# A 64-graph stack of two graph layers in a software pipeline: new orders for its first and last rows, and its last norm moved to VectorE

## The chip, the cores and the metric

The kernel runs on one core of a Trainium2 chip. The metric is the device time of one execution in microseconds. A profiled execution has its own time and a span, the time from its first to its last instruction. A core has five engines with a queue each: TensorE (PE in the profile, its weight loads PEld), VectorE (DVE), ScalarE (ACT), GpSimd (POOL) and SyncE (SP), which here issues nearly all DMA transfers. Each queue runs in the order in which it was written.

## The reference, cut to what matters

There are 64 independent graphs of 256 nodes with 256 features. Each passes through two layers, all in float32:

```python
# layer 0, per graph
h = gat(x, adj, W1, a1); h = gat(h, adj, W2, a2)        # gat: softmax of masked scores @ (h @ W)
h = layernorm(x + h, g_ln1, b_ln1)
x = layernorm(h + relu(h @ w_ff1 + b_ff1) @ w_ff2 + b_ff2, g_ln2, b_ln2)
# layer 1, per graph: 8 heads of 32, 4 relations (adj has 0 and 1 only)
attn = softmax(q @ k.T / sqrt(32))
out = sum(attn * (adj == r) @ (x @ Wv[r] + bv[r]) for r in range(4)) @ Wo + bo
x = layernorm(x + out, g1, beta1)
x = layernorm(x + gelu(x @ W1 + b1) @ W2 + b2, g2, beta2)
```

The layer norm subtracts the mean of each row, multiplies by 1/sqrt(variance + 1e-5), then by g, and adds b.

## The kernel before

The work on one graph is cut into pieces, small Python functions that issue a few instructions each. A piece has a name of stage and step. Stage G is the two attention steps of layer 0 (`G.wh` products with the joint weights `wx`, `G.e`, `G.lr`, `G.ad`, `G.ex` the scores, their maximum and exponentials, `G.gA` and `G.gB` the two weighted sums). Stage F is layer 0's norm and feed-forward (`F.ha` to `F.he` are the matmuls of the first product, seven block products in place of eight; `F.hk` copies by ACT and `F.hp` adds by VectorE collect them; `F.f0` and `F.f1` are the second product) and q and k. Stage A is the attention of layer 1: `A.sc0` and `A.sc1` the scores of four heads each, then for each head `mx`, `ex`, `rz`, `sp` (VectorE, ACT, VectorE, POOL), `dt` and `dm` (a transpose by DMA and its regrouping, issued by SP), `mg` (a copy) and `pm` (times adj); `A.v` the values, `A.o` the weighted sums. Stage T is the output product `T.wo`, the third norm, the gelu feed-forward and the last norm. Every norm has the pieces `ln` (sum and statistics, VectorE), `rs` (root, POOL), `nm` (scaling to y, VectorE), and `ra` and `rb` (times g, plus b, POOL). After the first three norms y also goes through a transpose by DMA (`dt`, `dm`) and a copy (`c`) into columns, and `s` forms block sums of them.

The order in which pieces are issued is written out by hand in `PERIOD` (lines 43 to 60): one row of pieces with a lag, `A.dt10/3` meaning that in period p the piece is issued for graph p-3. Lags go from 0 to 5, so up to six graphs are in work. The loop at line 791 runs 69 periods; in the first five and the last five it uses the same row and leaves out the graphs that don't exist yet or any more:

```python
        for period in range(B + max(lag for _, lag in order)):
            ...
            for piece, lag in order:
                if do := graphs.get(period - lag, {}).pop(piece, None):
                    do()
            after(period)
```

The setup stands outside of this. `joint_weights` makes `wx` from W1, W2 and the attention vectors (one product, and VectorE products and reductions). `column_bias` (line 168) folds a norm's bias into the bias of the next product by matmuls with one column, and `scale_rows` (line 162) multiplies a norm's weight into the rows of the next weight; `differences` (line 153) makes block differences of a weight on POOL. For the first feed-forward, q and k this is written ahead of the first piece (lines 260 to 268); for the values and the second feed-forward, with the loads of their weights, it follows the rows of periods 1 and 2 (`after`, line 307). `xT` and `x` have one buffer each, `adj` four, and PSUM's eight banks are shared in turn.

Of the kernel before, what the change touches and what calls it, by code (L numbers as in the profile page):

```python
# [25 lines left out]
F32 = mybir.dt.float32  # L26
# [4 lines left out]
AF = mybir.ActivationFunctionType  # L31
ALU = mybir.AluOpType
AX = mybir.AxisListType

P = 128
# [18 lines left out]
L.x/0 F.dmA/1 T.sC/4 F.ke0/2 F.rbB/3 T.hp1/4 F.ke1/2 A.sp02/3 A.vp2/3 T.rsD/5 F.q/2 A.pm10/3  # L54
F.qe0/2 T.nmD/5 F.sB/2 T.hb/4 G.rzA/0 A.ve/3 F.qe1/2 T.hk2/4 A.vk4/3 A.sc1/2 T.hc/4 A.dm00/3
A.mx12/2 F.cA/1 A.ex12/2 A.mx10/2 F.sA/1 A.ex10/2 A.mx11/2 A.rz12/2 A.rz10/2 A.mg00/3 A.dt02/3
T.raD/5 A.pm00/3 A.dt13/3 A.ex11/2 F.ha/1 F.hb/1 A.sp12/2 A.dm02/3 G.gA0/0 F.hk1/1 F.hk2/1 T.hk3/4
F.hp1/1 G.gA1/0 T.rbD/5 G.wd0/0 A.mx13/2 F.hc/1 G.wd1/0 G.eB/0 A.sp10/2 A.mg02/3 A.dm13/3 A.dt12/2
T.out/5 A.rz11/2 T.hp3/4
""".split()  # L60


@with_exitstack
# [24 lines left out]
def binary(ctx: ExitStack, tc: tile.TileContext, t, most, out: bass.AP):  # L88

    nc = tc.nc  # L90
# [18 lines left out]
    def mm_tile(name, shape=(P, 2, 256)):  # L109
        return psum.tile(list(shape), F32, tag="mm", name=name, bufs=8)  # L110

    def nodes(i):
        return slice(i * P, (i + 1) * P)
# [48 lines left out]
    def scale_rows(w, norm):  # L162

        for c in range(KC):
            for part in w(c):
                nc.vector.tensor_scalar_mul(part, part, norm[0][:, c : c + 1])

    def column_bias(bias, norm, block, n):

        ps = mm_tile("fold", (P, n))  # L170
        for i in range(n):
            for c in range(KC):
                nc.tensor.matmul(
                    ps[:, i : i + 1], block(c, i), norm[1][:, c : c + 1],
                    start=i == 0 and c == 0, stop=i == n - 1 and c == KC - 1,
                    skip_group_check=True,
                )
        nc.vector.tensor_tensor(bias, bias, ps, ALU.add)

    def fold_ff(f, bias, norm):  # L180

        half = FC // 2
        column_bias(
            bias, norm, lambda c, i: f[:, BLOCKS[c, i // half], i % half * P : (i % half + 1) * P], FC
        )
        scale_rows(lambda c: [f[:, BLOCKS[c, h], :] for h in range(2)], norm)

    def ff_factors(name):
        return half_factors(
# [67 lines left out]
    w1, differences = ff_factors("L0_gnn_w_ff1")  # L257
    ff0 = w1, column("L0_gnn_b_ff1"), weight("L0_gnn_w_ff2", FC)
    rows = {n: row(t[n], n) for n in ("L0_gnn_g_ln1", "L0_gnn_b_ln1", "L0_gnn_b_ff2")}
    fold_ff(w1, ff0[1], norms[0])  # L260
    differences()
    norms.append((column("L0_gnn_g_ln2"), column("L0_gnn_b_ln2")))
    wk, wq = (weight(f"L1_gnn_{n}", KC) for n in ("Wk", "Wq"))
    bk, bq = column("L1_gnn_bk"), column("L1_gnn_bq")
    for w, bias in ((wk, bk), (wq, bq)):
        column_bias(bias, norms[1], lambda c, i, w=w: w[:, c, nodes(i)], KC)
        scale_rows(lambda c, w=w: [w[:, c, :]], norms[1])
    nc.gpsimd.tensor_scalar(bq, bq, QSCALE, 1.0, ALU.mult, ALU.mult)
    rows |= {n: row(t[n], n) for n in ("L0_gnn_g_ln2", "L0_gnn_b_ln2", "L1_gnn_bo")}
    rows |= {f"bv{r}": row(t["L1_gnn_bv"][r], f"bv{r}") for r in range(2)}  # L270
    bv0 = const.tile([P, KC], F32, name="col_bv0")
# [3 lines left out]
    norms.append((column("L1_gnn_g1"), column("L1_gnn_beta1")))  # L275
    late = {}

    def fold_values():

        for c in range(KC):  # L280
            one, zero = (wv[:, BLOCKS[c, h], :] for h in (1, 0))
            nc.gpsimd.tensor_tensor(one, one, zero, ALU.subtract)
        column_bias(bv0, norms[1], lambda c, i: wv[:, BLOCKS[c, 0], nodes(i)], KC)
        ps = mm_tile("fold", (P, D))
        for c in range(KC):
            nc.tensor.matmul(
                ps, norms[1][1][:, c : c + 1].to_broadcast([P, P]), wv[:, BLOCKS[c, 1], :],
                start=c == 0, stop=c == KC - 1,
            )
        join_biases(("bv1", "bv0", ALU.subtract))  # L290
        nc.vector.tensor_tensor(rows["bv1"], rows["bv1"], ps, ALU.add)
        scale_rows(lambda c: [wv[:, BLOCKS[c, h], :] for h in range(2)], norms[1])
        value_differences()

    def join_biases(*pairs):

        for b, bias, *op in pairs:
            nc.vector.tensor_tensor(rows[b], rows[b], rows[bias], *op or [ALU.add])

    def late_weights():  # L300
        w1, late["differences"] = ff_factors("L1_gnn_W1")
        late["wo"] = weight("L1_gnn_Wo", KC)
        late["ff1"] = w1, column("L1_gnn_b1"), weight("L1_gnn_W2", FC)
        for n in ("L1_gnn_g1", "L1_gnn_beta1", "L1_gnn_b2", "L1_gnn_g2", "L1_gnn_beta2"):
            rows[n] = row(t[n], n)

    def after(period):

        if period == 1:
            fold_values()  # L310
            late_weights()
            join_biases(("L0_gnn_b_ln1", "L0_gnn_b_ff2"), ("L0_gnn_b_ln2", "L1_gnn_bo"))
        elif period == 2:
            fold_ff(*late["ff1"][:2], norms[2])
            late["differences"]()
            join_biases(("L1_gnn_beta1", "L1_gnn_b2"))

    def over_nodes(name):
        return rows[name].unsqueeze(1).to_broadcast([P, NT, D])
# [31 lines left out]
        return join  # L351


    def layernorm(do, stage, key, name, src):

        tiles = {}

        def sums():
            ps, residual = src()
            acc = tiles["acc"] = work.tile([P, NT, D], F32, tag="acc", name=f"acc_{name}", bufs=2)  # L360
            nc.vector.tensor_tensor(acc, ps, residual, ALU.add)
            stats = small.tile([P, NT, 6], F32, tag="stats", name=f"stats_{name}", bufs=2)
            mv = tiles["mv"] = small.tile([P, NT, 2], F32, tag="mv", name=f"mv_{name}")
            for i in range(NT):
                nc.vector.bn_stats(stats[:, i, :], acc[:, i, :])
                nc.vector.bn_aggr(mv[:, i, :], stats[:, i, :])
            tiles["var"] = small.tile([P, NT], F32, tag="var", name=f"var_{name}")
            nc.vector.tensor_scalar_add(tiles["var"], mv[:, :, 1], EPS)

        def root():  # L370
            tiles["rstd"] = small.tile([P, NT], F32, tag="rstd", name=f"rstd_{name}")
            nc.gpsimd.tensor_tensor(tiles["rstd"], tiles["var"], neghalf, ALU.pow)

        def norm():
            y = tiles["y"] = work.tile([P, 2, KC, NT, 64], F32, tag="y", name=f"y_{name}", bufs=3)
            for i in range(NT):
                nc.vector.tensor_scalar(
                    y[:, :, :, i, :],
                    tiles["acc"][:, i, :].rearrange("p (k c d) -> p c k d", k=KC, c=2),
                    tiles["mv"][:, i, 0:1], tiles["rstd"][:, i : i + 1], ALU.subtract, ALU.mult,  # L380
                )

        do[f"{stage}.ln{key}"], do[f"{stage}.rs{key}"], do[f"{stage}.nm{key}"] = sums, root, norm
        return tiles

    def scaled(do, stage, key, name, tiles, g, b):
# [375 lines left out]
    def graph(b, do, tiles):  # L762
        a = gat(do, b, tiles)
        to_columns(do, "F", "A", f"a{b}", a, "ACT")
        scaled(do, "F", "A", f"a{b}", a, "L0_gnn_g_ln1", "L0_gnn_b_ln1")
        combine(do, "F", "A", f"a{b}", a)
        feed_forward(do, "F", f"a{b}", a, lambda: ff0, "r", AF.Relu)
        y = layernorm(do, "F", "B", f"b{b}", lambda: (a["ff"], a["res"]))
        to_columns(do, "F", "B", f"y{b}", y, "ACT")
        scaled(do, "F", "B", f"b{b}", y, "L0_gnn_g_ln2", "L0_gnn_b_ln2")  # L770
        combine(do, "F", "B", f"y{b}", y)
        heads = attention(do, b, projections(do, b, y), tiles)
        c = layernorm(do, "T", "C", f"c{b}", lambda: (heads["wo"], y["res"]))
        to_columns(do, "T", "C", f"c{b}", c, "ACT")
        scaled(do, "T", "C", f"c{b}", c, "L1_gnn_g1", "L1_gnn_beta1")
        combine(do, "T", "C", f"c{b}", c)
        feed_forward(do, "T", f"c{b}", c, lambda: late["ff1"], "ge", AF.Gelu)
        d = layernorm(do, "T", "D", f"d{b}", lambda: (c["ff"], c["res"]))
        scaled(do, "T", "D", f"d{b}", d, "L1_gnn_g2", "L1_gnn_beta2")

        def store():
            nc.sync.dma_start(out=out[b].rearrange("(t p) d -> p t d", p=P), in_=d["res"])

        do["T.out"] = store
# [2 lines left out]
    E = mybir.EngineType  # L787
    graph(0, graphs[0], tiles[0])
    order = [(piece, int(lag)) for piece, lag in (entry.split("/") for entry in PERIOD)]
    with tc.manual_schedule(engines={E.PE, E.DVE, E.Activation, E.Pool, E.SP}):  # L790
        for period in range(B + max(lag for _, lag in order)):
            if 0 < period < B:
                graphs[period] = {}
                graph(period, graphs[period], load(graphs[period], period))
            for piece, lag in order:
                if do := graphs.get(period - lag, {}).pop(piece, None):
                    do()
            after(period)
        assert not any(graphs.values()), graphs


@with_exitstack
# [289 lines left out]
```

## Time and profile before

| | |
|---|---|
| median of 3 runs | 3156.15 us (3155.87 to 3160.32) |
| the profiled execution's own time | 3158.29 us |
| its span | 3156.4 us |
| granted TensorE clock, mean | 0.986 |
| busy share of PE, DVE, ACT, POOL | 97%, 78%, 81%, 67% |
| mean busy share of the 16 DMA engines, 400 to 2800 us | 0.73 to 0.76 |

A row of the profile names the line of the kernel, the engine, the operation and the tiles that it writes and reads (buffer numbers left out, so `hX_a` stands for that tile of every graph), then counts and durations; a bracket gives the idle time of the engine just before and what ended it. In the rows `ff_a` and `ff_c` are the second products of the two feed-forwards, `hX`, `hY`, `hZ` their first products, `fold` the matmuls of `column_bias`, `wh` the product with `wx`, `res_d` the output.

### The profile page before, as it was taken

How to read it: one execution, taken by the hardware profiler on the slowest of the kernel's cores; microseconds unless marked ns; L12 is line 12 of the kernel's file. 1: busy time of each engine (PE TensorE's matmuls, PEld its weight loads, DVE VectorE, ACT ScalarE, POOL GpSimd, SP SyncE). 2: the span in 40 equal slices, each digit the busy share in tenths (PEclk: the TensorE clock that was granted, in tenths of full speed). 3: DMA queues.
4: the chain of work that ended last, by engine and by line, in shares of the span. 5: the costliest groups of instructions: out<-in, count | busy, mean ns of one | idle time of the engine just before them, and what ended most of it. 6: DMA issues, size and time to landing. Idle time of an engine off the chain costs nothing.

```text
span 3156.4 us, 64811 instructions
## 1 busy us (share of the span) xinstructions
PE 3048.8 (97%) x21734; PEld 2613.1 (83%) x21734; DVE 2459.1 (78%) x5231; ACT 2555.5 (81%) x5822; POOL 2122.4 (67%) x2990
## 2 busy tenths in 40 slices
PE   5799999999999999999999999999999999999996
PEld 4678888888888888888888888888888888888875
DVE  3578888888888888888887888888888888888763
ACT  1478888888888888888888888888888888888874
POOL 2457667667766766766766776766776676676664
PEclk8899999999999999999999999999999999999998
DMA  4477777778678677777677777777777767777663
GB/s 133 87 140 151 142 148 147 146 142 153 145 148 151 143 143 154 144 148 147 146 143 150 148 145 146 151 141 149 151 143 147 152 141 148 151 143 145 143 128 68
DMA packets 1022849, 449.14 MB, mean 142 GB/s; under 512 B 770960, under 2 KB 1020816, under 8 KB 1022512
## 3 DMA queue, kind: packets, MB, share of 16 engines
q1 hardware_dynamic: 1021248, 442.70, 70.0%
q8 instruction: 175, 2.87, 0.4%
q0 software_dynamic: 976, 1.72, 0.4%
q14 instruction: 162, 1.33, 0.1%
q10 hardware_dynamic: 288, 0.52, 0.1%
HBM read 58.87 MB, written 16.78 MB: 24 GB/s over the span
## 4 chain that ended last, share of the span: by engine, by line
PE 85%; DMA 5%; ACT 3%; DVE 3%; POOL 2%; issue 2%; SPq 0%; ACTq 0%; POOLq 0%; DVEq 0%
PE ff_a L517 13%; PE ff_c L517 12%; PE o L721 7%; PE hX_a L495 7%; PE hX_c L495 6%; PE sc L671 4%; PE vX L645 3%; PE k L632 3%; PE wo L740 3%; PE wh L544 3%; PE q L632 3%; PE gat_b L597 3%; PE hY_c L495 3%; PE gat_a L597 3%; PE hY_a L495 3%; DMA halves_p<-pairs_p 3%
## 5 line engine op out<-in xcount | busy, mean ns | idle before, releaser
L345 ACT COPY pm<-halves_p 128x1024 uint16<-128x1024 uint16 x384 | 516.6, 1346 | 119.6 <-DMA halves_p<-pairs_p 118.6
L713 DVE TENSOR_TENSOR pm<-pm,adj 128x512 f32<-128x512 f32 x512 | 465.4, 926 | 87.4 <-POOL pm L345 63.6
L517 PE MATMUL ff_c<-w_L_gnn_W,hid_c 128*128 128x256 f32 x2048 | 466.2, 381 | 8.4 <-ACT hid_c L509 8.4
L517 PE MATMUL ff_a<-w_L_gnn_w_ff,hid_a 128*128 128x256 f32 x2048 | 455.0, 380 | 2.2 <-ACT hid_a L509 2.2
L517 PEld LDWEIGHTS ff_a<-w_L_gnn_w_ff,hid_a 128*128 128x128 f32 x2048 | 390.6, 191 | 56.4 <-ACT hid_a L509 2.9
L517 PEld LDWEIGHTS ff_c<-w_L_gnn_W,hid_c 128*128 128x128 f32 x2048 | 385.9, 191 | 61.2 <-ACT hid_c L509 10.2
L721 PE MATMUL o<-pm,v 128*32 128x256 f32 x4096 | 249.9, 383 | 1.3 <-ACT pm L345 0.9
L509 ACT ACTIVATE hid_a<-hid_a,col_L_gnn_b_ff 128x256 f32<-128x256 f32 x512 | 218.4, 512 | 12.4 <-DVE hid_a L477 12.4
L345 POOL COPY pm<-halves_p 128x1024 uint16<-128x1024 uint16 x128 | 172.1, 1345 | 81.5 <-DMA halves_p<-pairs_p 74.7
L509 ACT ACTIVATE hid_c<-hid_c,col_L_gnn_b 128x256 f32<-128x256 f32 x512 | 218.3, 496 | 4.9 <-DVE hid_c L477 2.0
L721 PEld LDWEIGHTS o<-pm,v 128*32 128x32 f32 x4096 | 120.7, 110 | 98.5 <-issue 16.7
L425 POOL TENSOR_TENSOR S_a<-cols_a 128x128 f32<-128x128 f32 x128 | 58.5, 457 | 179.2 <-ACT cols_a L345 179.2
L495 PEld LDWEIGHTS hX_a<-cols_a,f_L_gnn_w_ff 128*128 128x128 f32 x1024 | 126.0, 194 | 41.4 <-DVE s_B L573 24.3
L495 PE MATMUL hX_a<-cols_a,f_L_gnn_w_ff 128*128 128x128 f32 x1024 | 144.6, 285 | 13.3 <-ACT cols_a L345 9.2
L671 PE MATMUL sc<-kT,qT 32*128 32x256 f32 x2048 | 149.1, 403 | 1.5 <-ACT qT L642 1.5
L495 PE MATMUL hX_a<-S_a,f_L_gnn_w_ff 128*128 128x128 f32 x1024 | 138.2, 278 | 9.1 <-ACT hid_a L474 9.0
L345 ACT COPY cols_y<-halves_y_y 128x1024 uint16<-128x1024 uint16 x64 | 86.5, 1352 | 74.5 <-DMA halves_y_y<-pairs_y_y 74.4
L632 PE MATMUL k<-cols_y,w_L_gnn_Wk 128*128 128x256 f32 x512 | 127.2, 393 | 18.5 <-ACT cols_y L345 18.5
L495 PE MATMUL hX_c<-S_c,f_L_gnn_W 128*128 128x128 f32 x1024 | 141.7, 281 | 2.2 <-ACT hid_c L474 2.2
L495 PEld LDWEIGHTS hX_a<-S_a,f_L_gnn_w_ff 128*128 128x128 f32 x1024 | 130.0, 192 | 16.7 <-ACT hid_a L474 12.6
L495 PEld LDWEIGHTS hX_c<-cols_c,f_L_gnn_W 128*128 128x128 f32 x1024 | 134.2, 191 | 11.6 <-ACT cols_c L345 4.2
L495 PEld LDWEIGHTS hX_c<-S_c,f_L_gnn_W 128*128 128x128 f32 x1024 | 124.2, 191 | 23.0 <-issue 19.6
(2747 smaller groups left out, 8837.6 us busy)
## 6 DMA issues: line engine op xcount, KB each, us to landing
halves_p<-pairs_p SPq DMA_DIRECT2D x1024, 128.0 KB, 3.3
xT<-in_xT SPq DMA_DIRECT2D x64, 256.0 KB, 4.0
adj<-in_adjT SPq DMA_DIRECT2D x64, 256.0 KB, 4.0
x<-in_x SPq DMA_DIRECT2D x64, 256.0 KB, 3.3
halves_y_a<-pairs_y_a SPq DMA_DIRECT2D x128, 128.0 KB, 3.3
halves_y_y<-pairs_y_y SPq DMA_DIRECT2D x128, 128.0 KB, 3.2
halves_y_c<-pairs_y_c SPq DMA_DIRECT2D x128, 128.0 KB, 3.0
out<-res_d SPq DMA_DIRECT2D x64, 256.0 KB, 2.4
```

The lines of the kernel that those rows point to most:

```text
L345: copy(into().bitcast(U16).rearrange("p (n s) -> p s n", s=2), t["halves"].rearrange("p s k q -> p s (k q)"),)
L495: nc.tensor.matmul(ps[:, f * P : (f + 1) * P], weights()[0][:, factor, f * P : (f + 1) * P], left, start=start and f == 0, stop=f == FC // ...
L509: nc.scalar.activation(tiles["hid"][:, f, :], tiles["hid"][:, f, :], func, bias=b1[:, f : f + 1])
L517: nc.tensor.matmul(tiles["ff"][:, i, :], tiles["hid"][:, f, nodes(i)], weights()[2][:, f, :], start=(f == 0), stop=(f == FC - 1),)
L544: nc.tensor.matmul(t["whp", j], tiles["xT"][:, c, nodes(j)], wx[:, c, :], start=(c == 0), stop=(c == KC - 1),)
L597: nc.tensor.matmul(ps, t["s"][:, j, nodes(i)], t["whz"][:, j, :width], start=(j == 0), stop=(j == NT - 1),)
L632: nc.tensor.matmul(t[key + "p"][:, o, :], w[:, c, nodes(o)], tiles["cols"][:, c, :], start=(c == 0), stop=(c == KC - 1),)
L645: nc.tensor.matmul(ps, left, wv[:, factor, :], start=start, stop=True, skip_group_check=True)
L671: nc.tensor.matmul(t["sc", g, hh][:, i, :], qkv["q"][hd, g, nodes(i)], qkv["k"][hd, g, :], start=True, stop=True,)
L713: nc.vector.tensor_tensor(pm[:, 1, :], pm[:, 0, :], tiles["adj"], ALU.mult)
L721: nc.tensor.matmul(ps[hh * DH : (hh + 1) * DH, :], qkv["v"][:, j, d0 : d0 + DH], t["pm", (g, hh)][:, r, j * N : (j + 1) * N], start=(r == ...
L740: nc.tensor.matmul(t["wo"][:, i, :], t["oT"][:, c, nodes(i)], late["wo"][:, c, :], start=(c == 0), stop=(c == KC - 1),)
```

## The change

There are now three orders. `START` is an order of its own for what the first five rows held: 447 entries like `F.ha:1`, a piece and its graph. Then follow 59 periods with `PERIOD`, as before but for one piece. `END` holds what the last five rows held, 466 entries with graphs counted from the end (`F.ha:-1`). The setup is cut into pieces named `S.`, which stand among START's entries: `S.f0`, `S.f1`, `S.f2` (fold, scaling and differences of the first feed-forward), `S.l0` to `S.l2` (the same of the second), `S.q0`, `S.q1` (fold and scaling for q and k, now with one PSUM tile for both), `S.v0` to `S.v3` (values), `S.lw` (loads of the late weights), `S.lr` (loads of the late rows and of one column), `S.j1`, `S.j2` (sums of bias rows). The loads of a graph are entries too, so that their place on SP's queue is free.

The last norm has other passes: `nm` computes (acc - mean) * g on VectorE, which doesn't need the root, `rb` multiplies by the root and adds b on VectorE, and `T.raD` is gone; y is not formed there.

```diff
 PERIOD = """
...
-T.raD/5 A.pm00/3 A.dt13/3 A.ex11/2 F.ha/1 F.hb/1 A.sp12/2 A.dm02/3 G.gA0/0 F.hk1/1 F.hk2/1 T.hk3/4
...
+START = """
+G.wh0:0 S.lr:0 G.away:0 G.wh1:0 L.adj:1 G.wc0:0 S.v0:0 L.xT:1 G.wc1:0 G.eA:0 G.lrA:0 G.adA:0
+S.f0:0 G.exA:0 G.rzA:0 S.f1:0 G.gA0:0 G.gA1:0 G.wd0:0 G.wd1:0 G.eB:0 G.lrB:0 G.adB:0 G.wh1:1
+G.wh0:1 G.exB:0 G.rzB:0 S.v1:0 S.f2:0 G.gB:0 G.wc0:1 L.xT:2 G.wh1:2 G.away:1 G.wc1:1 G.lnA:0
+S.q0:0 G.rsA:0 G.eA:1 G.wh0:2 G.nmA:0 G.wc0:2 F.dtA:0 G.lrA:1 G.adA:1 G.exA:1 F.dmA:0 G.rzA:1
+G.gA1:1 L.adj:2 L.xT:3 G.gA0:1 F.cA:0 S.lw:0 G.wd0:1 F.ha:0 S.v2:0 G.wc1:2 S.j1:0 F.hk1:0 F.sA:0
...
+G.wc0:3 G.rsA:1 F.dtB:0 G.nmA:1 F.dmB:0 F.cB:0 G.gA0:2 F.dtA:1 F.dmA:1 S.q1:0 S.l0:0 G.wd0:2 F.q:0
+F.k:0 F.qe0:0 F.raA:1 F.qe1:0 F.ke0:0 F.sB:0 G.wh1:3 F.ke1:0 S.l1:0 A.sc1:0 A.mx11:0 F.cA:1 F.ha:1
...
+END = """
+A.pm02:-4 A.sp11:-3 A.dm12:-3 A.dt10:-3 F.hk3:-2 A.pm01:-4 G.lrB:-1 F.raA:-2 T.hd:-5 A.mg13:-4
...
+T.ge2:-3 A.dt01:-1 T.ge3:-3 A.dm02:-1 A.pm00:-1 A.dm01:-1 T.raC:-4 T.ha:-2 T.sC:-2 A.vp2:-1
...
+T.rsD:-2 T.nmD:-3 T.rbD:-3 T.ge0:-1 T.ge1:-1 T.he:-1 T.hk4:-1 T.ge2:-1 T.ge3:-1 T.f0:-1 T.f1:-1
+T.out:-3 T.nmD:-2 T.rbC:-1 T.rbD:-2 T.lnD:-1 T.nmD:-1 T.rsD:-1 T.rbD:-1 T.out:-2 T.out:-1
...
-    fold_ff(w1, ff0[1], norms[0])
-    differences()
...
-    for w, bias in ((wk, bk), (wq, bq)):
-        column_bias(bias, norms[1], lambda c, i, w=w: w[:, c, nodes(i)], KC)
-        scale_rows(lambda c, w=w: [w[:, c, :]], norms[1])
-    nc.gpsimd.tensor_scalar(bq, bq, QSCALE, 1.0, ALU.mult, ALU.mult)
...
+    setup = {
+        "S.f2": differences, "S.q0": queries, "S.q1": scaled_queries,
+        "S.v0": value_difference, "S.v1": values, "S.v2": scaled_values, "S.v3": value_differences,
+        "S.lw": late_weights, "S.lr": late_rows, "S.l2": lambda: late["differences"](),
...
+        def weighted():
+
+            tiles["res"] = work.tile([P, NT, D], F32, tag="res", name=f"res_{name}", bufs=3)
+            for i in range(NT):
+                nc.vector.scalar_tensor_tensor(
+                    tiles["res"][:, i, :], tiles["acc"][:, i, :], tiles["mv"][:, i, 0:1],
+                    rows[last[0]], ALU.subtract, ALU.mult,
+                )
+
+        def finished():
+            for i in range(NT):
+                nc.vector.scalar_tensor_tensor(
+                    tiles["res"][:, i, :], tiles["res"][:, i, :], tiles["rstd"][:, i : i + 1],
+                    rows[last[1]], ALU.mult, ALU.add,
+                )
...
     with tc.manual_schedule(engines={E.PE, E.DVE, E.Activation, E.Pool, E.SP}):
...
+        for entry in START:
+            piece, b = entry.split(":")
+            run(piece, int(b))
+        for period in range(lags, B):
             for piece, lag in order:
...
+                run(piece, period - lag)
+        for entry in END:
+            piece, b = entry.split(":")
+            run(piece, B + int(b))
```

## The prediction

> **What bounds the kernel now.** I read the page first (shares, the 40 slices), then the busy times by stretch, then the timeline of each end, then the groups of the middle. The page:
>
> ```profile
> span 3156.4 us, 64811 instructions
> ...
> PE 3048.8 (97%) x21734; PEld 2613.1 (83%) x21734; DVE 2459.1 (78%) x5231; ACT 2555.5 (81%) x5822; POOL 2122.4 (67%) x2990
> ...
> PE   5799999999999999999999999999999999999996
> PEclk8899999999999999999999999999999999999998
> ```
>
> TensorE is full in all slices but the first three and the last. So the middle is its work, and only the ends have room. By stretch (columns: stretch, length, busy us of PE, PEld, DVE, ACT, POOL, granted clock, DMA share, GB/s):
>
> ```profile
> 0.00:30.40 30.40, 14.09 (x56) 12.82 (x57) 9.87 (x28) 1.28 (x1) 10.74 (x22) 1.00 0.70 190
> 30.40:111.97 81.57, 47.92 (x183) 38.85 (x183) 34.87 (x76) 23.20 (x59) 23.83 (x35) 0.75 0.34 83
> 111.97:213.75 101.78, 86.12 (x566) 72.59 (x567) 69.59 (x146) 67.06 (x170) 61.60 (x89) 0.90 0.66 125
> 213.75:2979.60 2765.85, 2760.32 (x19944) 2375.02 (x19943) 2251.95 (x4781) 2355.46 (x5370) 1930.10 (x2711) 1.00 0.74 147
> 2979.60:3058.50 78.90, 74.09 (x532) 61.50 (x530) 54.06 (x117) 61.67 (x133) 53.52 (x78) 0.98 0.63 128
> 3058.50:3156.40 97.90, 66.26 (x458) 52.28 (x458) 38.81 (x87) 46.85 (x93) 42.58 (x59) 0.88 0.39 81
> ```
>
> I cut at 213.75, where period 5 begins (its first matmuls are T.hd of graph 0), and at 2979.60, 59 periods later. In the timeline the undisturbed period is 46.65 us; 59 of them are 2752.4, so the middle holds 13.5 us of small waits. The start takes 213.75 us, of which busy time times clock is about 14+36+78=128 at most; the end takes 176.8 us, with 72.6+58.3=131. Together 131 us of the ends are not matmul work at full clock: the most that any order could return, and never all of it, since the first graph has nothing to overlap with and the last has nobody behind it. The lines that set the ends:
>
> ```profile
> 23.38 0.48 DVE L166 TENSOR_SCALAR f_L_gnn_w_ff<-f_L_gnn_w_ff,col_L_gnn_g_ln 128x512 f32<-128x512 f32 x1 [3.41 <-PE fold L173]
> 29.52 0.14 DVE L249 COPY wx<-wa 128x1 f32<-128x1 f32 x1
> 30.46 3.76 PE L544 MATMUL wh<-wx,xT 128*128 128x260 f32 x8
> 95.00 1.91 PE L544 MATMUL wh<-wx,xT 128*128 128x260 f32 x8
> 111.97 1.15 PE L671 MATMUL sc<-kT,qT 32*128 32x256 f32 x16 [0.99 <-ACT qT L642]
> 158.83 1.15 PE L671 MATMUL sc<-kT,qT 32*128 32x256 f32 x16 [0.50 <-ACT qT L642]
> 204.36 1.15 PE L671 MATMUL sc<-kT,qT 32*128 32x256 f32 x16
> 3128.42 1.16 PE L495 MATMUL hX_c<-cols_c,f_L_gnn_W 128*128 128x128 f32 x8 [3.77 <-ACT cols_c L345]
> ```
>
> wx, which every graph's first product needs, is finished at 29.5 because VectorE's queue holds scalings of the first feed-forward weights, which wait for a load and for the fold. Then A.sc1 of graphs 0, 1 and 2 stand 46.9 and 45.5 us apart: nearly a full period each, at 59% and 82% of a period's work. These are chains, not loads of work.
>
> **The change, part by part.**
>
> *Setup out of the front.* After the wait for adj at 15.12, VectorE has `away` (0.35), four products and four reductions (0.60 each, start to start), `most` (0.60) and small copies (0.5): 6.3 us, so wx at 21.4 and the first wh at 21.5, 9 us earlier. The fold S.f0 (6.56 us for 30 of its matmuls in the cold timeline) now stands behind e_A of graph 0, inside the 5 us that gat_a waits for the exponentials; about 1.5 sticks out. S.v1 and the wh products of graph 1 (1.9 and 1.7 us warm, twice that cold) stand before gat_b: +3. So F.ha of graph 0, at 65.4 now, comes at about 61.
>
> *From there to A.sc1:0*, 46.6 us now. The chain alone: products to second matmul 13 (the pieces at 0.9 with copies of 0.6 and adds of 0.7 between), 6.9 for F.f0 and F.f1, 12.3 from there to the columns (12.06 at 93.4 now, 13.4 at the end), 4.9 for k, q and sc (481.0 to 485.9): 37 us at full clock. Here the clock decides. The row: eight wh matmuls take 3.76 us at 30 and 1.91 at 95, and the clock in 30 to 112 is 0.75. The Trainium skill, "TensorE: Matmul & The Clock Gate", Part 1, says the array runs at half rate until it was busy for one window of about 3.4 us, and falls back after an idle one. By that rule the fillers (44 us of warm matmul work now stand ahead of A.sc1:0) keep it warm, and the piece costs 37; with the row's 0.75 kept, fillers lengthen the chain and it costs some 44. Sum by the one 3110, by the other 3117; I take 40, nearer the row's middle: A.sc1:0 at 101, 11 earlier.
>
> *Graphs 1 and 2.* In START, F.ha:1 follows A.sc1:0 and F.ha:2 follows A.sc1:1, so the same 37 us chain plus sc (1.1) sets the distance; matmul work between is 26 and 35, which fits. I take 39.5 for each, against 46.9 and 45.5: 13.4 gained. One cause is visible: POOL's differences for the second feed-forward (L155, 1.4 and 4.2 us at 124.9 to 131) hold up the scaling of the first heads, and with S.l2 they come after graph 0's heads. The last 9.4 us stay. Start: about 24.5.
>
> *Moved queues.* S.lr puts its six loads on POOL's queue at the front (0.55 to 0.9 us each, some 5 in all, a few waits for landing as at 9.12): POOL's next needed work is S.v0 and S.f2 (1.6 and 5.1 us), wanted only at 42 and 61, so nothing; without that cover, 5 us. S.lw puts six loads (2.25 MB, some 5 us of issue and 10 at the 218 GB/s of the first slice) on SP before x of graph 1 and y_b's transposes, which come 15 us later; now they also lie in front of the second layer's first transposes. Nothing; uncovered, up to 10 on graph 0. START also reorders the loads of adj, xT and x of graphs 1 to 4 on SP; they land 4.0 and 3.3 us after issue and are wanted later: nothing, 4 if one is late. S.q1 and S.l1 (4 us of VectorE) lie in the wait for columns. bq's scaling goes from POOL to VectorE, 0.2 us.
>
> *End.* END moves T's products and second matmuls of older graphs behind the last graphs' F and A. Ahead of F.ha:-1 stand 36.3 us of matmul work (counting pieces at their steady times), then the 37 us chain: A.sc1:-1 at 73.4 after the end's start, 83.9 now (3063.5): 10.5. From there to the last o, 49.4 now with 33 of work on any engine and 10 transposes; the held-back T work fills it, the chain of heads limits it: 45, 4.5 gained. The 41 us from there to the end keep their order.
>
> *The output's norm.* The last lines of the chain:
>
> ```profile
> 3147.14 0.70 POOL L372 TENSOR_TENSOR rstd_d<-var_d,neghalf 128x2 f32<-128x2 f32 x1 [11.38 <-DVE var_d L368]
> 3148.37 1.51 POOL L392 TENSOR_TENSOR res_d<-y_d,row_L_gnn_g 128x256 f32<-128x256 f32 x2 [0.53 <-DVE y_d L377]
> 3149.95 1.26 POOL L399 TENSOR_TENSOR res_d<-res_d,row_L_gnn_beta 128x512 f32<-128x512 f32 x1
> ```
>
> Now: root, y_d, two products, one add, store at 3151.24. After: the first VectorE pass runs beside the root, the second ends at about 3148.7: 2.5 us gained at the end. End: about 17.5.
>
> *In the middle* each graph loses 3.2 us on POOL (2x957 + 1277 ns) and two scalings on VectorE (543 ns), and gains four two-input passes of 128x256. No row shows them; the nearest is the 128x512 one (groups of 412 to 2800), s_B 682 ns and s_A 953 beside POOL:
>
> ```profile
> L573 DVE SCALAR_TENSOR_TENSOR s_A<-s_A 128x512 f32<-128x512 f32 x51 | 48.6, 953 | 5.9 <-ACT s_A L568 5.9
> L573 DVE SCALAR_TENSOR_TENSOR s_B<-s_B 128x512 f32<-128x512 f32 x51 | 34.8, 682 | 0.0
> ```
>
> Half of it with its fixed part is 0.41 (as v<-v,vX, 128x256), 0.57 contended: +0.55 to +1.2 per graph. VectorE is idle 8.7 of 46.9 us. "SBUF — State Buffer" of the skill, on the shared port pair, speaks against the change: a VectorE op with two SBUF inputs and a POOL op that reads exclude each other for the whole instruction. By it each pass may stand 1.28 us behind an add, +5.7 per graph; by the row +1.2. The second pass sits before A.mx13, and hid_a's adds behind it feed F.he, which has 2.1 us of slack, and 0.7 more from an add's own wait: 2.8. By the row the pair takes 1.1, and nothing shows; I take zero. Below zero the POOL relief could remove some of the 13.5 us of waits, but those are ACT's waits for DMA, so at most 3.
>
> **Sum.** 24.5+17.5+0 = 42 off the profiled span of 3156.4. The profiled execution took 3158.3, 1.9 outside the span and 2.1 above the median of the runs; the saving goes on the median 3156.15: 3114.
>
> **Rivals.**
> - *Chains as now (A), 0.48*: 3114, own range 3099 to 3128.
> - *The ends pack better (B), 0.24*: work alone allows it. From A.sc1:0 on the start has 69.6 busy us on VectorE and 67.1 on ACT (third stretch), and by count 69 of matmuls, in 101.8; at 92% that is 76, with A.sc1:0 at 97: start 40 off, end 30 off, 3086. Against it: the 37 us chain three times in a row.
> - *Cold clock and in-order waits (C), 0.18*: setup folds hold gat_b and q in the cold array, spacing stays 44: start 10 off, end 10 off, 3136.
> - *It doesn't do what it says, 0.04*: a START entry blocks a queue until its load lands, giving back what is gained: 3150 to 3162.
> - *Slower, 0.06*: the second pass of the norm meets POOL's adds by the lock rule in every period. Above 2.8 us the pair delays F.he; from 3.5 us the loss (0.7x59) eats the 42. Blocked by an add and by a pair of p's scalings it takes 0.8+1.3+1.9 = 4.0, 1.2 too long: 71 us lost, 3185. For: y_d itself is 543, not 400, beside POOL. Against: no L573 pass more than 40% slow on average.
>
> A measurement of this kernel can tell 0.2% (6.3 us) from no change. Faster by more: A, B, C and a little: 0.91; within: 0.03; slower: 0.06. The range takes A, most of B and C: 3083 to 3138.
>
> **What would show it.** wx's last copy near 21, first wh right after; A.sc1 of graphs 0 to 2 at about 101, 140, 180; period 5 (T.hd:0) at 189; a period of 46.65 with no PE wait behind VectorE's adds into hid_a; the last o near 118 after the end's start; store 1.6 us after rstd_d begins. Wrong if wx isn't earlier, if the spacing stays 46, or if PE waits for VectorE in each period.

## The result and the profile after

The changed kernel takes 3127.4 us (median of 4 runs, 3124.2 to 3130.0) against 3157.7 for the kernel before beside it: a ratio of 0.9903, with a 95% interval of 0.9886 to 0.9920. That is some 30 us gained where 42 were forecast. The profiled execution took 3128.74 us, its span is 3126.6. First the page:

```profile
span 3126.6 us, 64671 instructions
...
PE 3041.8 (97%) x21734; PEld 2606.9 (83%) x21734; DVE 2470.3 (79%) x5360; ACT 2554.7 (82%) x5820; POOL 1976.6 (63%) x2797
...
PE   6889999999999999999999999999999999999987
```

POOL has 146 us less to do and the first slices are fuller. The busy times by stretch say more (stretch, length, PE, PEld, DVE, ACT, POOL, granted clock, DMA share, GB/s). The stretches begin and end at the same pieces as before: first `wh`, A.sc1 of graph 0, T.hd of graph 0, T.hd of graph 59, A.sc1 of the last graph:

```profile
0.00:21.81 21.81, 3.75 (x8) 2.52 (x8) 6.58 (x18) 1.28 (x1) 14.08 (x27) 1.00 0.91 215
21.81:96.84 75.03, 62.17 (x278) 52.10 (x278) 37.69 (x90) 23.09 (x61) 22.25 (x30) 0.86 0.39 111
96.84:196.79 99.95, 80.09 (x518) 64.67 (x519) 65.42 (x139) 65.51 (x167) 55.31 (x79) 0.93 0.57 118
196.79:2953.30 2756.51, 2754.14 (x19945) 2373.09 (x19944) 2264.30 (x4902) 2360.73 (x5371) 1803.88 (x2546) 1.00 0.73 147
2953.30:3035.86 82.56, 71.65 (x525) 60.27 (x523) 53.83 (x116) 61.29 (x133) 45.54 (x70) 0.96 0.60 123
3035.86:3126.60 90.74, 70.01 (x466) 54.23 (x466) 42.45 (x98) 42.77 (x90) 35.51 (x47) 0.92 0.40 84
```

The start is 196.79 us long instead of 213.75 (17.0 gained, 24.5 forecast). The 59 periods of the middle take 2756.51 instead of 2765.85 (9.3 gained, zero forecast). The end takes 173.3 instead of 176.8 (3.5 gained, 17.5 forecast). So the forecast gain was 12 us too large: by 14 in the end and by 7.5 in the start, less the middle's 9, which it lacked. That the time lies inside the stated range (3083 to 3138) is in part luck: without the middle's 9 us it would have been some 3137, one us inside.

The timeline of TensorE has the start's milestones (start, us, engine, operation, in brackets the idle time before and what ended it):

```profile
21.81 3.94 PE L683 MATMUL wh<-wx,xT 128*128 128x260 f32 x8 [9.59 <-DVE wx L352]
96.84 1.15 PE L810 MATMUL sc<-kT,qT 32*128 32x256 f32 x16
138.19 1.15 PE L810 MATMUL sc<-kT,qT 32*128 32x256 f32 x16 [0.93 <-ACT qT L781]
187.76 1.15 PE L810 MATMUL sc<-kT,qT 32*128 32x256 f32 x16
```

The first product comes at 21.8, as worked out. A.sc1 of graph 0 comes at 96.8 (101 was said), of graph 1 41.4 us later (39.5), of graph 2 another 49.6 later (39.5). The last distance is the one that failed.

Two more lines of this timeline bear on the account below: the folds of `S.l0`, matmuls with one column, and right behind them `q` of graph 0, which takes 3.78 us where the same product takes 1.89 in the middle:

```profile
85.09 3.80 PE L265 MATMUL fold<-col_L_gnn_beta,f_L_gnn_W 128*128 128x1 f32 x32
89.26 3.78 PE L771 MATMUL q<-cols_y,w_L_gnn_Wq 128*128 128x256 f32 x8 [0.38 <-ACT cols_y L463]
```

The row of that stretch shows a granted clock of 0.50:

```profile
88.40:95.20 6.80, 6.42 (x17) 5.17 (x18) 2.36 (x5) 1.88 (x4) 5.00 (x8) 0.50 0.37 116
```

### The profile page after: what moved, and what is told of

Read it like the earlier page. It is cut to its first block, busy times and chain, and to the rows that moved or that the text cites. A ratio compares the mean times of both kernels' runs of the same rounds, so it can differ in the third digit from the quotient of the medians.

```text
span 3126.6 us, 64671 instructions
## 1 busy us (share of the span) xinstructions
PE 3041.8 (97%) x21734; PEld 2606.9 (83%) x21734; DVE 2470.3 (79%) x5360; ACT 2554.7 (82%) x5820; POOL 1976.6 (63%) x2797
## 4 chain that ended last, share of the span: by engine, by line
PE 91%; DMA 4%; ACT 2%; DVE 1%; issue 1%; POOL 1%; SPq 0%; ACTq 0%; POOLq 0%; DVEq 0%
PE ff_a L656 13%; PE ff_c L656 13%; PE o L860 7%; PE hX_a L634 7%; PE hX_c L634 7%; PE sc L810 4%; PE vX L784 4%; PE q L771 3%; PE k L771 3%; PE wh L683 3%; PE gat_a L736 3%; PE hY_a L634 3%; PE gat_b L736 3%; PE wo L879 3%; PE hY_c L634 3%; DMA halves_p<-pairs_p 2%
## 5 line engine op out<-in xcount | busy, mean ns | idle before, releaser
L463 ACT COPY pm<-halves_p 128x1024 uint16<-128x1024 uint16 x384 | 516.2, 1345 | 69.1 <-DMA halves_p<-pairs_p 68.4
L852 DVE TENSOR_TENSOR pm<-pm,adj 128x512 f32<-128x512 f32 x512 | 401.1, 801 | 85.5 <-POOL pm L463 64.4
L683 PE MATMUL wh<-wx,xT 128*128 128x260 f32 x512 | 135.9, 389 | 14.6 <-DVE wx L352 9.6
L634 PE MATMUL hX_c<-cols_c,f_L_gnn_W 128*128 128x128 f32 x1024 | 137.3, 278 | 8.8 <-ACT cols_c L463 7.5
L491 POOL TENSOR_TENSOR rstd_b<-var_b,neghalf 128x2 f32<-128x2 f32 x64 | 44.8, 699 | 157.7 <-DVE var_b L487 151.8
L491 POOL TENSOR_TENSOR rstd_c<-var_c,neghalf 128x2 f32<-128x2 f32 x64 | 51.0, 796 | 145.6 <-DVE var_c L487 140.4
```

Of the source, the lines that this page charges most:

```text
L463: copy(into().bitcast(U16).rearrange("p (n s) -> p s n", s=2), t["halves"].rearrange("p s k q -> p s (k q)"),)
L634: nc.tensor.matmul(ps[:, f * P : (f + 1) * P], weights()[0][:, factor, f * P : (f + 1) * P], left, start=start and f == 0, stop=f == FC // ...
L683: nc.tensor.matmul(t["whp", j], tiles["xT"][:, c, nodes(j)], wx[:, c, :], start=(c == 0), stop=(c == KC - 1),)
L852: nc.vector.tensor_tensor(pm[:, 1, :], pm[:, 0, :], tiles["adj"], ALU.mult)
```

## The experiments

Theory D, formed on the traces: what the forecast's sum lacked is the transposes by DMA. A transpose goes through a tile `pairs` (filled by the DMA transpose) and a tile `halves` (filled by the regrouping DMA), and each has two buffers. A graph needs 11 transposes per period: 8 heads and three norms. `pairs` is held from the issue of the transpose until the halves have landed. The changed kernel's chain of waits in the end shows one such passage (start, us, what):

```profile
2996.41 3.08 DMA pairs_p<-p
2999.55 0.54 SPq L456
3000.14 3.09 DMA halves_p<-pairs_p
```

That is some 7 us. Two buffers then pass one transpose per 3.5 us, an estimate from these rows, so 11 take 38.5 of the 46.65 us of a period: 82%. Over 412 to 2800 us of the same trace the time from issue to landed halves is longer, a mean of 8.0 us for a head and of 7.0 to 7.8 for a norm. That makes 86 us per period for two buffers, a resource used to 92%. The rivals were that START's order, not the norm, empties the middle's waits, and that pieces in front of the last graph's pieces, in queues that run in order, make the end long.

The runs, by ratio to the kernel before beside them:

| kernel | median, us | ratio | 95% interval |
|---|---|---|---|
| norm_only | 3149.7 | 0.9980 | 0.9973 to 0.9987 |
| start_only | 3145.4 | 0.9963 | 0.9949 to 0.9977 |
| end_only | 3154.4 | 0.9991 | 0.9983 to 0.9999 |
| pool_back | 3176.5 | 1.0056 | 1.0043 to 1.0069 |
| pairs3 | 3107.3 | 0.9845 | 0.9829 to 0.9862 |
| start_j2 | 3121.1 | 0.9886 | 0.9870 to 0.9903 |
| start_l2 | 3126.6 | 0.9903 | 0.9886 to 0.9919 |
| end_f | 3129.6 | 0.9914 | 0.9897 to 0.9930 |
| before_pairs3 | 3140.1 | 0.9940 | 0.9923 to 0.9956 |
| pairs3_halves2 | 3113.2 | 0.9851 | 0.9835 to 0.9868 |
| pairs3_j2 | 3104.4 | 0.9826 | 0.9810 to 0.9842 |
| pairs3_j2_endf | 3114.8 | 0.9859 | 0.9842 to 0.9875 |

And the same four distances in the trace of each, in us. They are read from the starts of `ff_a`, the first layer's second feed-forward product: of graph 0; from graph 0 to graph 5; from graph 5 to graph 58, less 53 undisturbed periods of 46.65; from graph 58 to the span's end.

| kernel | ff_a of graph 0 | 0 to 5 | 5 to 58, excess | 58 to the end |
|---|---|---|---|---|
| before | 84.0 | 233.8 | 11.2 | 355.0 |
| after | 70.1 | 232.5 | 2.1 | 349.4 |
| norm_only | 83.1 | 234.1 | 6.5 | 355.3 |
| start_only | 69.2 | 230.1 | 13.3 | 357.5 |
| end_only | 84.0 | 235.0 | 8.9 | 353.0 |
| pool_back | 69.6 | 233.0 | 47.0 | 354.0 |
| start_j2 | 67.5 | 228.8 | 2.2 | 350.0 |
| start_l2 | 70.1 | 232.1 | 2.8 | 349.4 |
| end_f | 68.8 | 230.7 | 3.4 | 353.1 |
| before_pairs3 | 83.5 | 232.6 | 0.1 | 349.4 |
| pairs3 | 69.1 | 224.4 | 0.1 | 339.2 |
| pairs3_halves2 | 69.4 | 226.0 | 0.1 | 343.5 |
| pairs3_j2 | 66.5 | 221.4 | 0.1 | 341.5 |
| pairs3_j2_endf | 69.6 | 221.7 | 0.3 | 348.4 |

With the same start, ff_a of graph 0 still differs by up to 3.5 us from one execution to the next (66.5 to 70.1), so differences of that size in one trace's sum count for little. The diffs of the orders below show the entries around a change, not whole lines.

### The three parts alone

`norm_only` takes the two passes into the kernel before:

```diff
-T.raD/5 A.pm00/3 A.dt13/3
+A.pm00/3 A.dt13/3
...
-        d = layernorm(do, "T", "D", f"d{b}", lambda: (c["ff"], c["res"]))
-        scaled(do, "T", "D", f"d{b}", d, "L1_gnn_g2", "L1_gnn_beta2")
+        d = layernorm(
+            do, "T", "D", f"d{b}", lambda: (c["ff"], c["res"]), ("L1_gnn_g2", "L1_gnn_beta2")
+        )
```

> The kernel before with the norm's two passes alone (T.raD gone, rbD on VectorE). Between T.hd of graph 0 and T.hd of graph 59 the changed kernel took 2756.5 us, the kernel before 2765.9: 9.3 less, where zero was forecast. Theory M (POOL's relief does it: 3.2 us less on POOL per graph lets the pieces behind it come earlier): 9 in the middle and 2 at the last store, so about 3146. Rival S (the start's order leaves the pipeline in a better state, which then lasts): only the 2 at the store, 3154, and the periods still vary between 46.65 and 47.6.

`start_only` has START and the setup pieces:

```diff
-        for entry in END:
-            piece, b = entry.split(":")
-            run(piece, B + int(b))
+        for period in range(B, B + lags):
+            for piece, lag in order:
+                if piece in graphs.get(period - lag, {}):
+                    run(piece, period - lag)
```

> START and the setup pieces alone; the last periods are PERIOD with the missing graphs left out, and the output's norm is the old one on POOL. T.hd of graph 0 came 17.0 us earlier in the changed kernel. Theory M: 17 from the start and nothing in the middle, 3139. Rival S: 17 and the 9 of the middle, 3130.

`end_only` has END, with `T.raD` put into it:

```diff
-        for period in range(B + max(lag for _, lag in order)):
+        for period in range(B):
...
+        for entry in END:
+            piece, b = entry.split(":")
+            graphs[B + int(b)].pop(piece)()
```

> END alone in the kernel before, with the old norm (T.nmD, T.raD in their order after T.rsD). The changed kernel's end is 173.3 us long, the old one 176.8, and some 2 of the 3.5 are the norm's. Theory E (END's order is worth 1.5 because the chain of the last heads through the transposes sets the end's length): 3154 to 3156. Rival (END as such is worth the 10 that were forecast, and the norm or the start takes it back): 3146.

The norm alone gives 6 us (4 to 9), and its trace loses 4.7 us of waits in the middle: less than theory M's 9, more than rival S's nothing. START alone gives 12 (7 to 16); its trace has ff_a of graph 5 18.5 us earlier (69.2 + 230.1 against 84.0 + 233.8), and the middle's waits are all still there (13.3 against 11.2). So rival S is wrong as it stood. END alone gives 3 (0 to 5), as theory E said. The three together give 0.97%, their parts add to 0.66%: some 10 us exist only in the combination, though the intervals leave room for 2 to 17. Part of that may be in the middle: the four traces that have START, the new norm, two buffers and no other POOL work show 2.1 to 3.4 of excess, the norm alone 6.5, in an execution that took 3.7 us more than its kernel's median. Why START helps there once the norm has changed is not settled.

### POOL's time

`pool_back` gives POOL the removed work back, all three instructions in one place, without use for the result:

```diff
+        def filler():
+            for i in range(NT):
+                nc.gpsimd.tensor_tensor(idle[:, i, :], idle[:, i, :], rows["L1_gnn_g2"], ALU.mult)
+            nc.gpsimd.tensor_tensor(idle, idle, over_nodes("L1_gnn_beta2"), ALU.add)
+
+        do["T.raD"] = filler
```

> The changed kernel with three idle POOL instructions per graph of the old shapes (two products 128x256, one add 128x512 on a scratch tile) put back where T.raD stood; the result does not use them. Theory M: the middle's 9 us come back, 3127 + 9 = 3136, and PE waits again for hid_a's copies. Rival S, and a rival Y (what helped is the freed y buffer or VectorE's shorter queue, not POOL's time): 3127 to 3129.

The direction is M's, the size five times as large: 49 us more than the changed kernel and 18 more than the kernel before. Rival S is out, and so is Y as the cause of the whole: START, the freed y and VectorE's shorter queue are all still there, and the waits are back. The size says that this isn't the old work in its old places, so the run shows the direction and not how much of the 9 us is POOL's. How it reaches TensorE is seen in the idle time of the copies that take a head out of `halves`. The view of that tile says, for 412 to 2800 us, how long the copying engines stood idle and until what; the four lines are those of before, after, pool_back and pairs3:

```profile
DMA halves_p<-pairs_p: 141.0, 153
```

```profile
DMA halves_p<-pairs_p: 50.4, 88
```

```profile
DMA halves_p<-pairs_p: 187.2, 163
```

```profile
DMA halves_p<-pairs_p: 22.6, 48
```

norm_only has 66.3. The order is that of the middle's excess: 11.2, 2.1, 47.0, 0.1, and 6.5. ACT and POOL stand for a transposed head, and the copies of `hid_a` stand behind them. POOL scales the heads (`sp`) before they may be transposed: a late POOL starts a late transpose, and with two buffers a late transpose also makes the next ones late.

There is a second way, and the two kernels' groups of the norm's second pass show it (engine, operation, shapes, count, busy us and mean ns), after and then pool_back, 412 to 2800 us:

```profile
L513 DVE SCALAR_TENSOR_TENSOR res_d<-res_d,rstd_d,row_L_gnn_beta 128x256 f32<-128x256 f32 x102 | 59.4, 621 | 0.0
```

```profile
L513 DVE SCALAR_TENSOR_TENSOR res_d<-res_d,rstd_d,row_L_gnn_beta 128x256 f32<-128x256 f32 x100 | 94.3, 981 | 0.0
```

With POOL busy beside it the pass takes 360 ns more per instruction. The groups of the pages say the same from the other side. `pm`, eight VectorE products per graph, before and after:

```profile
L713 DVE TENSOR_TENSOR pm<-pm,adj 128x512 f32<-128x512 f32 x512 | 465.4, 926 | 87.4 <-POOL pm L345 63.6
```

```profile
L852 DVE TENSOR_TENSOR pm<-pm,adj 128x512 f32<-128x512 f32 x512 | 401.1, 801 | 85.5 <-POOL pm L463 64.4
```

125 ns eight times is 1.0 us per graph that VectorE got back, two thirds of the 1.5 us that its new passes cost beyond the two scalings that they replace. It comes with the norm (795 ns in norm_only, 922 in start_only). In pool_back, where the same POOL work stands in another place, `pm` takes 825: so what counted was the work that stood beside `pm`, more than POOL's total. How the 47 us of pool_back are split between late transposes and slower VectorE passes isn't told apart; that POOL's work came in one piece there, not in two, may add to it.

### Three buffers for the transposes

```diff
-            t["pairs"] = work.tile([P, 2, 4, P], U16, tag="pairs", name=f"pairs_{name}", bufs=2)
+            t["pairs"] = work.tile([P, 2, 4, P], U16, tag="pairs", name=f"pairs_{name}", bufs=3)
...
-            t["halves"] = work.tile([P, 2, 4, P], U16, tag="halves", name=f"halves_{name}", bufs=2)
+            t["halves"] = work.tile([P, 2, 4, P], U16, tag="halves", name=f"halves_{name}", bufs=3)
```

> The changed kernel with three buffers each for pairs and halves (the two stages of every transpose) instead of two. In its last 173 us SyncE stood 14.8 us at the issue of a transpose until halves of two transposes before had landed. Theory D (two buffers make the transposes of the last heads a chain, and that chain, not the order of the pieces, sets the end): end from 173.3 to about 165, and a few us of the start, 3117 to 3121; the middle is at its floor and stays. Rival O (the lists issue one transpose ahead of each pair of halves anyway, so a third buffer finds nothing to do): 3125 to 3129.

3107.3: 20 us less than the changed kernel's 3127.4 (18 by the ratios), more than theory D asked; rival O is out. The waits of SyncE's queue show where (engine and line, what it waited for, us, times, longest). In 412 to 2800 us of the changed kernel, its largest wait is the issue of a transpose (L448) for a buffer to come free:

```profile
SPq L448 <- DMA halves_p<-pairs_p: 173.1, 204, 2.1
...
SPq L448 <- POOL p L837: 110.9, 125, 2.7
```

In pairs3 the first of these lines is gone from the list, and the transposes wait for their data:

```profile
SPq L448 <- POOL p L837: 275.9, 152, 4.3
```

The middle's excess is gone (0.1 us over 53 periods), the end is 10.2 us shorter, and the way from graph 0 to graph 5 8.2 shorter. The kernel before gets the same two buffers:

> The kernel before with three buffers each for pairs and halves, nothing else. Theory D (two buffers made the transposes a chain in every stage, whatever the order): the middle goes to its floor (11 us), the end loses some 8, the start a few: 3133 to 3137. Rival (the 20 us that the third buffers gave the changed kernel need its new orders, and the old lists find nothing to do with them): 3150 to 3155.

3140.1, three us above theory D's interval: the middle is at its floor (11.1 gained, as said), the end 5.6 shorter (8 said), the start hardly (1.6). So the buffers limited the kernel before too. And since its middle reaches the floor with POOL's old work still in place, POOL's relief has nothing left to give there once a third buffer exists. Which of the two tiles is scarce:

> The changed kernel with three buffers for pairs only, two for halves. In its end SyncE stood 14.8 us at transposes until halves had landed (this frees pairs) and about 5 us at halves until a copy by ACT or POOL was done (this frees halves). If pairs is the scarce one: 3107 to 3112. If halves is: 3120 or more.

3113.2 with `pairs` alone, just above the interval: `pairs` brings the whole middle and 14 of the 20 us by the medians, 16 of 18 by the ratios. What the third `halves` buffer adds, 6 or 2 us, is not clear of noise; the traces put it in the two ends (1.6 and 4.3 us).

### Graph 2 in the start

```diff
-S.v2:0 G.wc1:2 S.j1:0 F.hk1:0
+S.v2:0 G.wc1:2 S.j1:0 S.j2:0 F.hk1:0
...
-L.adj:4 A.dm10:1 S.j2:0 A.mx00:1
+L.adj:4 A.dm10:1 A.mx00:1
```

> One entry of START moved: S.j2:0 right behind S.j1:0. The tile joined lies in one of the eight pm buffers until S.j2; the eighth head of graph 0 therefore got a buffer that A.o1:0 was still to read, and POOL's copy stood 4.4 us for it, with VectorE's hid_a add of graph 2 behind. Theory B (this buffer wait is the main part of graph 2's long spacing of 49.6): ff_a of graph 2 at 154 instead of 158, T.hd of graph 0 at 193 instead of 196.8, 3123 to 3124. Rival: what is gained there is lost again in front of q of graph 2, where VectorE has its queue full; 3127.

In the changed kernel's timeline of POOL and then VectorE:

```profile
150.37 1.32 POOL L463 COPY pm<-halves_p 128x1024 uint16<-128x1024 uint16 x1 [4.44 <-PE o L860]
151.72 0.93 DVE L852 TENSOR_TENSOR pm<-pm,adj 128x512 f32<-128x512 f32 x1 [3.58 <-POOL pm L463]
```

and in that of start_j2 the same copy:

```profile
143.48 1.34 POOL L462 COPY pm<-halves_p 128x1024 uint16<-128x1024 uint16 x1
```

The wait is gone, and from ff_a of graph 0 to that of graph 5 the trace is 3.8 us shorter (4 said). 3121.1 is 5 to 6 below the changed kernel, though the intervals of the two ratios overlap; 2.5 us of the trace's difference lie ahead of graph 0's ff_a, where the edit only adds a short VectorE pass, and are not the edit's (69.6 in pairs3_j2_endf, with the same START). A.sc1 of graph 2 now stands 45.9 us behind that of graph 1 instead of 49.6, so theory B holds for 4 of the 10 us that graph 2 was late. The other cause that I saw was POOL's block differences beside VectorE:

```diff
-T.rsC:0 S.l2:0 A.dm01:1
+T.rsC:0 A.dm01:1
...
-A.mx13:1 A.mx11:1 F.sA:2
+A.mx13:1 A.mx11:1 S.l2:0 F.sA:2
```

> One entry of START moved: S.l2:0 (four POOL differences, 5.2 us) ahead of F.sA:2, where POOL was idle for 8.7 us. In the changed kernel it ran at 163.0 to 168.2, and VectorE's whz_B and y_c beside it took 2.65 and 1.67 us instead of about 1.1 and 0.9. Theory P (POOL's pass slows VectorE's, and acc_b of graph 2 waits for both): q of graph 2 2.4 us earlier, 3125. Rival: VectorE's chain there is given by its order and by the transposes; no change, 3127.

VectorE in the changed kernel, then in start_l2:

```profile
164.42 2.65 DVE L730 TENSOR_SCALAR whz_B<-wh_B,grz_B 128x256 f32<-128x256 f32 x2
168.67 0.66 DVE L480 TENSOR_TENSOR acc_b<-ff_a,res_a 128x512 f32<-128x512 f32 x1
```

```profile
164.42 0.62 DVE L729 TENSOR_SCALAR whz_B<-wh_B,grz_B 128x256 f32<-128x256 f32 x2
165.67 0.67 DVE L479 TENSOR_TENSOR acc_b<-ff_a,res_a 128x512 f32<-128x512 f32 x1
```

The contention was real, 2.65 us against 0.62, and acc_b starts 3.0 us earlier. But y_b starts only 0.9 earlier (170.60, 171.54 before), and q of graph 2 0.7 earlier (182.08 against 182.81). 3126.6 is no change: the rival's verdict. In start_l2 VectorE stands 2.4 us ahead of y_b for a head's exponentials (`p`, by ACT), so its order took back what acc_b had gained. The transposes have a share in that stretch, since pairs3 takes 3.9 us from the distance of graphs 1 and 2 (ff_a 49.1 to 45.3) and 2.2 from the next.

### The end's order

```diff
-F.hk3:-1 A.pm01:-3 F.hp1:-1 A.mg13:-3
+F.hk3:-1 A.pm01:-3 F.hp1:-1 F.hd:-1 F.hp3:-1 F.hp2:-1 F.r0:-1 F.he:-1 F.hk4:-1 F.r1:-1 F.r2:-1 F.r3:-1 A.mg13:-3
...
-A.o1:-3 F.r1:-1 A.o0:-3
+T.hd:-4 T.hp2:-4 T.hp3:-4 F.f0:-1 F.f1:-1 A.o1:-3 A.o0:-3
...
-T.dtC:-3 A.pm01:-2 A.sp03:-2 A.ex02:-2 F.dtB:-1
+F.dtB:-1 T.dtC:-3 A.pm01:-2 A.sp03:-2 A.ex02:-2
...
-T.dmC:-3 A.vk3:-2 T.cC:-3 F.dmB:-1 T.ha:-3 A.pm10:-2 T.hk4:-4 F.cB:-1
+F.dmB:-1 T.dmC:-3 A.vk3:-2 F.cB:-1 T.cC:-3 A.pm10:-2 T.hk4:-4
...
-F.q:-1 F.k:-1 T.hk1:-3
+F.q:-1 F.k:-1 T.ha:-3 T.hk1:-3
```

> END with the last graph's pieces put first: F.hd, F.hp3, F.hp2, F.r0 to F.r3, F.he, F.hk4 right behind F.hp1, F.f0 and F.f1 (with T.hd, T.hp2, T.hp3 of the graph three before it) ahead of A.o1:-3 and A.o0:-3, F.dtB, F.dmB and F.cB ahead of the pieces of T.C:-3, and T.ha:-3 behind F.k:-1. Theory Q (in-order queues: the last graph waits behind copies of heads that are still on their way through the transposes): ff_a of the last graph 6 us earlier, A.sc1:-1 at 74 to 76 after the end's start instead of 82.6, and the end some 5 shorter, 3121 to 3123. Theory D (the transposes of the heads set the end): A.sc1:-1 earlier, the last o not, 3125 to 3128.

3129.6: nothing gained, perhaps lost. ff_a of the last graph did start 7.9 us earlier (224.8 us after that of graph 58, against 232.7), yet A.sc1 of that graph came 40.6 us after it instead of 26.1. The wait had only changed its queue. VectorE's timeline of end_f:

```profile
3013.52 0.69 DVE L479 TENSOR_TENSOR acc_c<-wo,res_b 128x512 f32<-128x512 f32 x1 [0.61 <-PE wo L878]
...
3019.82 0.66 DVE L479 TENSOR_TENSOR acc_b<-ff_a,res_a 128x512 f32<-128x512 f32 x1
```

F.f0 and F.f1 now run ahead of T.wo:-3, but on VectorE F.lnB:-1 (acc_b) still stands behind T.lnC:-3 (acc_c), which needs that T.wo: acc_b starts 12.5 us after the last `ff_a` is over (3007.3), where in the changed kernel VectorE stood ready and waited 0.4 us for it. So this run doesn't decide between theories Q and D: my edit moved TensorE's and ACT's order and not VectorE's. It does show that the order alone can bring the last graph's ff_a 7.9 us forward.

### The edits together

`pairs3_j2` has the diffs of pairs3 and start_j2:

> Three buffers each for pairs and halves, and S.j2:0 right behind S.j1:0. The wait for joined's buffer and the transposes are different causes, if theory B holds: 3107.3 less most of the 6.3 that S.j2 alone gave, 3101 to 3103. If the third buffers already took that wait away: 3107.

3104.4: of the 6 us of S.j2, 3 are left beside the third buffers by the medians and all 6 by the ratios. This is the fastest kernel here, 0.8% below the changed kernel by the ratios; that it is faster than pairs3 is likely but not clear of noise, as the two intervals overlap.

`pairs3_j2_endf` has the diff of end_f as well:

> As pairs3_j2, with END's order of end_f, which alone brought the last graph's feed-forward 10 us forward and the end nothing. If only the transposes stood against it: 3 to 6 less than pairs3_j2, 3096 to 3099. If the last heads' own work (exponentials, scalings, copies) sets the end by now: the same as pairs3_j2 within 2.

3114.8, 10 us worse than pairs3_j2, outside both expectations. VectorE's queue shows the same block as in end_f: acc_b starts at 3008.99, and the last ff_a was over at 2996.5. What END is worth in its best order stays open.

## Why the prediction was right and where it was wrong

- **wx and the first product.** Right: 21.81 (21.5 said).
- **From F.ha:0 to A.sc1:0.** Right in number, by luck in part: F.ha:0 at 60.0 (61), the piece 36.8 us long, A.sc1:0 at 96.8 (101). I had weighed the row (44) against the rule of the Trainium skill, "TensorE: Matmul & The Clock Gate", Part 1 (37), and taken 40. The 37 came out, but not for its reason, that the fillers keep the array warm. The granted clock in the piece is 0.85 (0.79 before), and q and most of k ran at 0.50 right behind the folds, as rival C had it for q. Two errors cancel: the way to F.f0 took 10.1 us instead of 13, that from k and q to sc 7.6 instead of 4.9.
- **Graphs 1 and 2.** The mis-sized term of the start. "The same 37 us chain plus sc sets the distance" gave 39.5 twice; measured 41.4 and 49.6, 12 us more, so by the prediction's own sign ("if the spacing stays 46") graph 2 failed. My chain had the arithmetic of one graph with free resources. Missing were the buffers that it shares with the graph before. With three buffers for the transposes (pairs3) the distances are 37.5 and 49.1, with S.j2 moved, which frees a `pm` buffer earlier, 41.5 and 45.9, with both 37.3 and 45.0. That is 8.7 of the 12 us; what still holds graph 2 is open.
- **Moved queues.** Nothing was said for nearly all, 4 for a late load of a graph. One came: wh of graph 4 waited 5.0 us at 122.8 for xT, ahead of k of graph 1 on TensorE. What that cost wasn't tried.
- **The end.** The step that failed: "then the 37 us chain: A.sc1:-1 at 73.4". F.ha:-1 came 37.2 us after the end's start, as said (36.3). The chain from there took 45.3, as in the kernel before (45.4), so A.sc1:-1 came at 82.6. The buffers are not the cause of that: with three the chain still takes 44.5 (A.sc1:-1 at 81.7). Of the 45.3, 19.3 lie ahead of F.f0, where 13 was said. In end_f, with the chain's pieces put forward, that part takes 11.4, so it was their place in the queues; whether the whole chain can take 37 stays open, as end_f lost the time again on VectorE. The heads, forecast at 45, took 48.8 (49.4 before). There the buffers are the cause: 41.4 with three.
- **The output's norm.** Right in mechanism and near in size. The root starts at 3120.19, the store is issued at 3121.99, 1.8 us later (1.6 said); from the root's start to the span's end 6.4 us instead of 9.3. From the last o to the span's end only 1.6 of these 2.9 are left in this trace (41.9 against 43.5), mainly because the last `ff_c` took 8.86 us at a granted clock of 0.81 instead of 7.17 at 1.00. In pairs3, with the same end, it took 7.17, and the way is 40.0. T.he of the last graph also waited 1.3 us (0.8 before) for adds into hid_c, which stood on VectorE behind the sum of another graph's norm.
- **The middle, zero.** Wrong: 9.3. I had allowed 3 at most, since the waits were "ACT's waits for DMA" and POOL not their cause. But POOL is ahead of the DMA: its scaling is what a transpose waits for. The step that failed is reading a wait's releaser as its cause. norm_only's trace has 4.7 of it, start_only's none; the rest came only with both.
- **The second pass.** The pair takes 1.24 us (1.1 said); by the exclusive port rule of the skill's "SBUF — State Buffer" it would have been up to 2.6 more. In the changed kernel the trace doesn't show that price, as POOL's adds of this norm are gone; in pool_back it does, 0.36 us per instruction. The slower rival named a real mechanism. That it didn't come fits with the change taking away the POOL work with which the passes would have collided: in the changed kernel each second pass takes 0.55 to 0.70 us, in pool_back up to 1.5.

As a value of the orders the 42 us of the start and the end were less wrong: between the traces of before_pairs3 and pairs3, both without the scarce buffer, START, END and the norm's tail are worth 14.5 + 8.3 + 10.1 = 33 us, none of it in the middle. The start's part, 22.8, is then near the 24.5 said, and what is left of the error is the end (10.1 for 17.5). In total, though, the change is worth the same with three buffers as with two: a ratio of 0.9845/0.9940 = 0.9904 against 0.9903. So the scarce buffer decided where the gain appeared, and hardly how large it was.

Two slips of the prediction changed nothing: the page's row has TensorE short of full in two slices at the front, not three, and 37 and 44 us in the place of 40 make 3111 and 3118, not 3110 and 3117.

## What to carry to other kernels

A chain's length taken from one undisturbed graph is too short where other graphs share its queues and buffers (45.3 us for 37 in the end): before forecasting the gain of a new order, count for each rotating tile how long one use holds a buffer, times the uses per period, divided by its buffers, and set that beside the period, as for an engine. A wait for a DMA is followed one step further back, to what let the DMA start: a free buffer or a late producer. When pieces are moved ahead in a written order, they have to move on every queue that the next step passes through, or the wait only changes its queue.

## What was not expected of the hardware

- A head's transpose, 128x1024 values of two bytes, landed a median of 3.3 us after its issue (3.1 to 6.3, in 412 to 2800 us of the changed kernel), its regrouping also 3.3 (2.6 to 5.2). So with two staging buffers the rate of transposes is set by latency, at a DMA share of 0.73 that shows nothing of it.
- VectorE's scaling of two 128x256 tiles took 0.62 us alone and 2.65 us beside POOL's differences of 128x512 elements (1.3 us each). Each of the two passes (1.38 and 1.35 us) ended 0.15 us after the difference that ran beside it. That agrees with the exclusive lock that the Trainium skill states in "SBUF — State Buffer" for the port pair which the two share.
- The clock column counts time without a clock record as full. The first record of the changed kernel's trace is at 37.2 us, and the column shows 1.00 up to there; yet the eight products at 8.48 us took 3.75 us and the eight `wh` at 21.81 took 3.94, against 1.89 and 1.93 later. The trace of pairs3, whose records begin at 12.7 us, shows 0.51 from 16 to 26 us, with the same 3.94 for `wh`. So the 1.00 of the first stretch is no measurement, in the kernel before (first record at 34.0 us) as little as in the changed one.
- One-column matmuls kept TensorE busy, and the clock fell to half all the same: in the changed kernel at 88.4 us, at the end of folds from 85.09 to 88.89, and in pairs3 at 29.8 us, at the end of folds from 26.10 to 29.87. That the single column is the cause isn't shown.
